# A four-layer graph network: engine orders from a repeating table, and the first three groups rearranged

## The chip, the core and the metric

One core of one Trainium2 chip runs the whole kernel. The time is the device time in microseconds (us) of one execution, and the median of several executions is compared. Five engines work side by side: TensorE (PE, matmuls and transposes into PSUM), VectorE (DVE), ScalarE (ACT), GpSimd (POOL) and SyncE (SP), whose queue issues all the DMAs of this kernel.

## The reference

128 graphs of 128 nodes with 512 features, float32, go through four layers. Each adds to x what its graph operation gives and normalises the rows.

```python
x = layernorm(x + relu(einsum('bnm,bmf,fc->bnc', dh * (A + I) * dh, x, W0) + b0))      # layer 0
q, k, v = x @ Wqk.T, x @ Wv.T          # layer 1: scores are masked by A and summed over a row,
x = layernorm(x + softmax(sum(q k^T / 8 * A, -1), axis=nodes) * v)
x = layernorm(x + relu(concat([x, (A @ x) / max(deg, 1e-6)]) @ W2.T))                  # layer 2
x = layernorm(x + L(A) @ (x @ W3 + b3))                                                # layer 3
```

## The kernel before

**Groups and layers.** Four graphs form a group, 32 groups in all (`NT`). Each group goes through the four layers; the loop at the end of the kernel function runs layer 0 and 1 of group t beside layer 2 and 3 of group t - 1, so a turn of that loop has one of each layer. `begin()` writes out groups 0 and 1, and group 2's layer 0, by hand.

**Products.** The weight products use a two-by-two scheme with seven products in place of eight, called B11, T1, B21, B22, T2, T3, T4. Sums of the left operand (`left_sums`, tiles agg0s, agg3s, xT1s) and of the weights (`outer_sums`, `weight_sums`) feed it. Layers 0 and 3 do it in `project` (PSUM tiles p_o), layer 1 in `l1_out` (p_v), and layer 2 applies the scheme twice, as four passes (`PASSES`) of seven products over accumulators p_2x, whose results are collected in the tiles y1 (its v) and y2 (its y). At the end of layer 2, `l2_out` writes for each of four graphs g a seed, y1 times a row factor, into a PSUM tile p_2g by ScalarE or VectorE, and TensorE adds the product of arT and y2 to it. Each product of two 128-row float32 tiles appears as two matmul records.

**Weights.** Layer 1's wv_sb and most of layer 2's (wb_sb, wa_sb, wc_sb) stay in SBUF. The tile wz_sb is shared in turn by layer 0's weights, the last part of layer 2's and layer 3's; after the first use each set is kept in DRAM (w0d, w2d, w3d) and `fetch` loads it in seven pieces, each of which waits for the last product that reads the old piece.

**What sets the order.** The kernel function calls recorders, and nothing is issued until `nc.emit()`. A `Plan` then holds all operations with an estimated duration. `schedule` works out for each one when it is due (`last`), going back from the end over its readers, and adds 100 ns times an entry of the hand-set table `EARLY`. `run` goes forward in planned time: on each engine it takes, among the operations whose inputs and buffers are there, the one that is due first. `MOVED` names operations that go to another engine than the one written down. The keys of both tables are made by `keys`: engine letter, tile name without the group number, and a count, so one entry holds for every group. The result is a fixed order of instructions on each engine; on the chip each engine runs its own in that order and waits on semaphores. Every instruction is recorded by one helper, so its line in the profile is always L460, and the tile names tell the rows apart.

**The start.** `load_weight` and `load_w2` fetch the weights, the latter by 64 small DMAs into wb_sb, wa_sb, wc_sb and wz_sb, once w0 and w3 have been stored. `w2_sums` forms layer 2's sums in these tiles and stores w2d. Layers 1 and 3 use weights whose output mean has been taken off (`centre`, `centre_row`), by VectorE reductions and subtractions on VectorE or GpSimd. `l1_out(0)` puts its result v1_0 in one of the three x buffers.

Of the kernel before, what the change touches and what calls it, by code (L numbers as in the profile page):

```python
# [32 lines left out]
STATS = False  # L33
EARLY = {
    "g:agg0:0": 86, "g:agg0s1:0": -9, "g:agg0s2:0": 119, "g:agg0s4:0": 323, "g:agg3:0": -34, "g:agg30:0": 49,
    "g:agg30s1:0": 93, "g:agg30s2:0": 80, "g:agg30s4:0": -89, "g:agg31:0": -413, "g:agg31s1:0": 10,
    "g:agg31s2:0": 251, "g:agg31s4:0": -88, "g:agg3s1:0": -120, "g:agg3s2:0": 22, "g:agg3s4:0": -318, "g:arT:0": 62,
    "g:arT:1": -359, "g:d:0": 569, "g:inner:0": -54, "g:inner:1": 47, "g:inner:2": -803, "g:inners1:0": 585,
    "g:inners1:1": -183, "g:inners2:0": 991, "g:inners2:1": -116, "g:inners4:0": -90, "g:inners4:1": 237,
    "g:last3o2_0:0": -956, "g:last3o2_0:1": -51, "g:last3o2_0:2": -224, "g:last3o3_0:0": -366, "g:last3o3_0:1": 433,  # L40
    "g:last3o3_0:2": -917, "g:last3o3_0:3": 629, "g:last3o3_1:0": -630, "g:last3o3_1:1": 138, "g:last4o2_0:0": 1012,
    "g:rs:0": -45, "g:rstdo0_0:0": 39, "g:rstdo0_0:1": -71, "g:rstdo0_1:0": -161, "g:rstdo0_1:1": 587,
    "g:rstdo3_1:0": 350, "g:rstdo3_1:1": 432, "g:v1_0:0": 318, "g:v1_0:1": 295, "g:v1_1:0": -218, "g:v1_1:1": -168,
    "g:v2_0:0": -165, "g:v2_1:0": 1445, "g:wa_sb": 56, "g:wb_sb": -132, "g:wc_sb": 200, "g:wz_sb": 303,
    "g:xT1:0": -225, "g:xT1s1:0": 1610, "g:xT1s2:0": 246, "g:xT1s4:0": -55, "g:xT2:0": -478, "g:xT2:1": -131,
    "g:xT2:2": 116, "g:xT2s1:0": 136, "g:xT2s1:1": -762, "g:xT2s2:0": -59, "g:xT2s2:1": 667, "g:xT2s4:0": -488,
    "g:xT2s4:1": -14, "s:agg0:0": -232, "s:agg0:1": 46, "s:agg0:2": -437, "s:agg0:3": 398, "s:agg3:0": -3638,
    "s:agg3:1": -430, "s:agg3:2": -69, "s:agg3:3": 136, "s:agg3:4": 61, "s:agg30:0": -153, "s:agg30:1": -305,
    "s:agg31:0": 172, "s:agg31:1": 228, "s:ana:0": -446, "s:arT:0": -3, "s:b0_sb": -185, "s:b3_sb": -253,
    "s:dme:0": -145, "s:e_sb": 2, "s:f_2x0:0": -26, "s:f_2x1:0": -284, "s:f_2x2:0": 3, "s:f_2x3:0": -1252,  # L50
    "s:f_o0:0": 120, "s:f_o3:0": -61, "s:f_o3:1": 1810, "s:f_v_0:0": 60, "s:f_v_1:0": 145, "s:p_2g_0:0": 165,
    "s:p_2g_1:0": 133, "s:p_2g_2:0": 589, "s:p_2g_3:0": 103, "s:p_2x0:0": -309, "s:p_2x0:1": 2768, "s:p_2x1:0": 477,
    "s:p_2x1:1": -115, "s:p_2x2:0": 130, "s:p_2x2:1": 233, "s:p_2x3:0": -185, "s:p_2x3:1": -154, "s:p_o0:0": -207,
    "s:p_o0:1": -24, "s:p_o0:2": 257, "s:p_o0:3": 252, "s:p_o3:0": -495, "s:p_o3:1": -134, "s:p_o3:2": -399,
    "s:p_o3:3": 29, "s:p_v_0:0": 37, "s:p_v_0:1": 427, "s:p_v_1:0": -59, "s:p_v_1:1": 655, "s:sa:0": 1, "s:sa:1": 48,
    "s:sa:2": -170, "s:sa:3": -253, "s:square_0_0:0": 219, "s:square_0_1:0": 177, "s:square_1_0:0": -251,
    "s:square_1_1:0": 474, "s:squareo2_0_0:0": -443, "s:squareo2_0_1:0": 848, "s:squareo2_1_0:0": -347,
    "s:squareo2_1_1:0": 201, "s:squareo3_0_0:0": -50, "s:squareo3_0_1:0": 457, "s:squareo3_1_0:0": 733,
    "s:squareo3_1_1:0": -12, "s:to_dram<x:0": 52, "s:to_dram<x:1": -172, "s:to_dram<x:2": -76, "s:to_dram<x:3": 324,
    "s:v0:0": 138, "s:v0:1": -520, "s:v0:2": -233, "s:v1:0": -335, "s:v1:1": 399, "s:v1:2": 544, "s:w0d": -498,  # L60
    "s:w2d": 281, "s:w3d": 433, "s:wa_sb": 198, "s:wb_sb": 162, "s:wc_sb": -241, "s:wqk_sb": 255, "s:wv_sb": -194,
    "s:wz_sb": 328, "s:x:0": -12, "s:x:1": 625, "s:x:10": -442, "s:x:11": 200, "s:x:12": 445, "s:x:13": -171,
    "s:x:14": 307, "s:x:15": -59, "s:x:2": 68, "s:x:3": 454, "s:x:4": -272, "s:x:5": -170, "s:x:6": -485,
    "s:x:7": 368, "s:x:8": 373, "s:x:9": 253, "s:xT1:0": 108, "s:xT1:1": -485, "s:xT1:2": 3, "s:xT1:3": -151,
    "s:xT1s_0:0": 153, "s:xT1s_0:1": -190, "s:xT1s_1:0": -127, "s:xT1s_1:1": -430, "s:xT1y_0:0": 64, "s:xT1y_0:1": 42,
    "s:xT1y_0:2": 135, "s:xT1y_0:3": 218, "s:xT1y_1:0": 141, "s:xT1y_1:1": -13, "s:xT1y_1:2": 15, "s:xT1y_1:3": 24,
    "s:xT2:0": 310, "s:xT2:1": 256, "s:xT2:2": 210, "s:xT2:3": 751, "s:xT2s_0:0": -40, "s:xT2s_0:1": 381,
    "s:xT2s_1:0": -191, "s:xT2s_1:1": -117, "s:xT2y_0:0": -236, "s:xT2y_0:1": -890, "s:xT2y_0:2": 317,
    "s:xT2y_0:3": 1574, "s:xT2y_1:0": 4, "s:xT2y_1:1": 244, "s:xT2y_1:3": 262, "s:y1:0": -50, "s:y1:1": -287,
    "s:ya:0": -330, "s:ya:1": -107, "s:ya:2": -697, "s:ya:3": 55, "t:p_2g_0:0": -246, "t:p_2g_1:0": 174,  # L70
    "t:p_2g_2:0": -200, "t:p_2g_3:0": 149, "t:p_2x0:0": 352, "t:p_2x0:1": 30, "t:p_2x0:2": 946, "t:p_2x0:3": -246,
    "t:p_2x0:4": 382, "t:p_2x0:5": 204, "t:p_2x0:6": 120, "t:p_2x1:0": 294, "t:p_2x1:1": 107, "t:p_2x1:2": -149,
    "t:p_2x1:3": -357, "t:p_2x1:4": -298, "t:p_2x1:5": 817, "t:p_2x1:6": 127, "t:p_2x2:0": -33, "t:p_2x2:1": 187,
    "t:p_2x2:2": 226, "t:p_2x2:3": 246, "t:p_2x2:4": -173, "t:p_2x2:5": 24, "t:p_2x2:6": -56, "t:p_2x3:0": 189,
    "t:p_2x3:1": 1006, "t:p_2x3:2": 223, "t:p_2x3:3": 320, "t:p_2x3:4": -136, "t:p_2x3:5": 237, "t:p_2x3:6": 356,
    "t:p_a0:0": 48, "t:p_a1:0": -152, "t:p_agg0_0:0": 635, "t:p_agg0_1:0": 403, "t:p_agg0_2:0": 31,
    "t:p_agg0_3:0": -384, "t:p_agg30_0:0": -152, "t:p_agg30_1:0": 248, "t:p_agg31_2:0": -11, "t:p_agg31_3:0": 68,
    "t:p_agg3_0:0": 766, "t:p_agg3_1:0": -517, "t:p_agg3_2:0": -889, "t:p_agg3_3:0": 242, "t:p_o0:0": 210,
    "t:p_o0:1": -990, "t:p_o0:2": 294, "t:p_o0:3": 1257, "t:p_o0:4": 676, "t:p_o0:5": 473, "t:p_o0:6": 579,
    "t:p_o3:0": -3306, "t:p_o3:1": 64, "t:p_o3:10": -240, "t:p_o3:11": -195, "t:p_o3:12": -175, "t:p_o3:13": 1090,  # L80
    "t:p_o3:2": -69, "t:p_o3:3": 207, "t:p_o3:4": 1976, "t:p_o3:5": 215, "t:p_o3:6": 645, "t:p_o3:7": 52,
    "t:p_o3:8": 187, "t:p_o3:9": 250, "t:p_sc:0": 107, "t:p_v_0:0": -764, "t:p_v_0:1": 308, "t:p_v_0:2": -150,
    "t:p_v_0:3": 906, "t:p_v_0:4": -231, "t:p_v_0:5": -802, "t:p_v_0:6": 596, "t:p_v_1:0": -87, "t:p_v_1:1": -8,
    "t:p_v_1:2": 90, "t:p_v_1:3": 180, "t:p_v_1:4": 470, "t:p_v_1:5": 19, "t:p_v_1:6": -34, "t:p_w:0": 358,
    "t:p_warm": 20, "t:p_ws:0": -194, "t:p_xT1_0:0": -130, "t:p_xT1_1:0": 78, "t:p_xT1_2:0": -45, "t:p_xT1_3:0": 18,
    "t:p_xT2_1:0": -3, "t:p_xT2_3:0": -198, "v:agg0:0": 260, "v:agg0:1": -192, "v:agg0s1:0": 27, "v:agg0s1:1": 117,
    "v:agg0s2:0": 240, "v:agg0s2:1": 22, "v:agg0s4:0": 43, "v:agg0s4:1": 281, "v:anT:0": 401, "v:anT:1": -116,
    "v:ana:0": -280, "v:ana:1": -301, "v:arT:0": -479, "v:b0_sb": 130, "v:b3_sb": -107, "v:bno0_0_0:0": 768,
    "v:bno0_0_1:0": 210, "v:bno0_1_0:0": 80, "v:bno0_1_1:0": -75, "v:bno3_1_1:0": 327, "v:bno3_1_1:1": -101,
    "v:deg:0": 422, "v:dh:0": -425, "v:dm:0": 236, "v:e_sb": 275, "v:inner:0": -237, "v:inner:1": 20,  # L90
    "v:inner:2": 994, "v:inner:3": -598, "v:last1o2_0:0": 466, "v:mean_b3": -42, "v:mean_w3": -128, "v:mean_wv": 4,
    "v:means_w3": 103, "v:means_wv": 26, "v:mn:0": 85, "v:mvo0_0:0": -254, "v:mvo0_0:1": 188, "v:mvo0_1:0": 20,
    "v:mvo0_1:1": 303, "v:mvo3_1:0": -173, "v:nhalf": 288, "v:nmro0_0:0": 447, "v:nmro0_1:0": -335, "v:rs:0": -240,
    "v:rsum:0": -3534, "v:scr:0": -701, "v:scr:1": 452, "v:scr:2": -222, "v:scr:3": -276, "v:u3:0": 240, "v:u3:1": 42,
    "v:u3:2": -40, "v:u3:3": 141, "v:u_o0:0": -207, "v:u_o0:1": 180, "v:v0:0": -35, "v:v0:1": -1085, "v:v1:0": 135,
    "v:v1:1": 201, "v:wa_sb": 617, "v:wc_sb": -873, "v:ws:0": -646, "v:wv_sb": -481, "v:wz_sb": -266, "v:x:0": -1020,
    "v:x:1": -470, "v:x:10": 202, "v:x:11": -70, "v:x:12": 283, "v:x:13": 906, "v:x:14": 576, "v:x:15": 293,
# [1282 lines left out]
```

## Time and profile before

| | us |
|---|---|
| median of 3 runs | 2434.84 |
| lowest and highest | 2434.82, 2438.7 |
| the profiled execution | 2437.22 |
| its span, first to last instruction | 2435.4 |

| engine | busy us of the span | share |
|---|---|---|
| PE | 2372.5 | 97% |
| DVE | 1761.9 | 72% |
| POOL | 1318.8 | 54% |
| ACT | 1138.6 | 47% |

The page also gives the 16 DMA engines' mean busy share, 59.9% for the main queue, and the TensorE clock granted, 0.995 of full speed on average. Its rows read: output tile, then what is read, with the shape, the count, the busy time, the mean of one in ns, and the idle time of the engine before them with what ended it. In the view in order of time a row has its start, its length, the engine and, in brackets, the idle time before it and its releaser. Matmul ends in the profile are modelled; their starts are not.

### The profile page before, as it was taken

The numbers are of one execution on the slowest core, as the hardware profiler recorded it, in microseconds if no ns is written. First come the engines' busy times: TensorE is split into PE (matmuls) and PEld (weight loads), VectorE is DVE, ScalarE is ACT, GpSimd is POOL, SyncE is SP. The second block draws the span as 40 slices with busy tenths as digits, with TensorE's granted clock in tenths as the row PEclk, the third lists the DMA queues.
The fourth block names the chain that finished last, engine by engine and source line by source line (L and its number), as shares of the span: only waits on it lengthen the run. The fifth ranks groups of instructions, "written<-read, shape, count | busy, mean of one in ns | idle before, by whom it ended". The sixth has DMA issues, their size and how long they took to land. (4 is left out here: it accounts for less than half of the span.)

```text
span 2435.4 us, 35420 instructions
## 1 busy us (share of the span) xinstructions
PE 2372.5 (97%) x11244; PEld 1923.1 (79%) x11244; DVE 1761.9 (72%) x3534; ACT 1138.6 (47%) x2495; POOL 1318.8 (54%) x1586
## 2 busy tenths in 40 slices
PE   7999999999999999999999999999999999999997
PEld 6677777887778887778877778877788777788776
DVE  7687777767777777777677777777776777776675
ACT  3344454444444444544444444445444445444444
POOL 3555556555555555565555555555655555655444
PEclk9999999999999999999999999999999999999999
DMA  5366656656566666565666566665666665665542
GB/s 165 122 168 186 176 160 201 176 165 191 166 180 185 176 172 192 154 195 173 172 187 170 172 191 174 172 194 158 184 183 169 187 174 161 201 175 161 171 117 75
DMA packets 490426, 417.36 MB, mean 171 GB/s; under 512 B 151808, under 2 KB 373504, under 8 KB 489856
## 3 DMA queue, kind: packets, MB, share of 16 engines
q1 hardware_dynamic: 490240, 415.09, 59.9%
q8 instruction: 91, 1.49, 0.3%
q14 instruction: 95, 0.78, 0.1%
HBM read 297.27 MB, written 117.70 MB: 170 GB/s over the span
## 5 line engine op out<-in xcount | busy, mean ns | idle before, releaser
L460 PE MATMUL p_o<-wz_sb,agg 128*128 128x256 f32 x2048 | 465.4, 379 | 3.4 <-DVE p_o L460 1.8
L460 PEld LDWEIGHTS p_o<-wz_sb,agg 128*128 128x128 f32 x2048 | 385.7, 190 | 56.2 <-DVE p_o L460 2.2
L460 PE MATMUL p_v<-wv_sb,xT 128*128 128x320 f32 x1024 | 296.3, 436 | 3.3 <-POOL wv_sb L460 2.6
L460 PEld LDWEIGHTS p_v<-wv_sb,xT 128*128 128x128 f32 x1024 | 195.6, 192 | 95.9 <-issue 9.8
L460 PEld LDWEIGHTS p_agg<-anT,x 128*128 128x128 f32 x2048 | 250.3, 193 | 23.7 <-DVE x L460 7.8
L460 PE MATMUL p_agg<-anT,x 128*128 128x128 f32 x2048 | 257.6, 277 | 7.8 <-DVE x L460 7.0
L460 PE MATMUL p_v<-wv_sb,xT1s 128*128 128x320 f32 x768 | 233.0, 433 | 0.0
L460 POOL TENSOR_TENSOR y<-u,y 128x1024 f32<-128x1024 f32 (+1 forms) x96 | 192.1, 2001 | 50.7 <-DVE y L460 40.9
L460 ACT COPY agg<-p_agg 128x512 f32<-128x512 f32 (+1 forms) x255 | 133.2, 535 | 164.9 <-PE p_agg L460 164.9
L460 PE MATMUL p_o<-wz_sb,agg0s 128*128 128x256 f32 x768 | 183.9, 383 | 6.6 <-DMA wz_sb<-w0d 5.7
L460 ACT COPY p_2x<-p_2x 128x512 f32<-128x512 f32 (+1 forms) x256 | 130.0, 518 | 127.2 <-PE p_2x L460 127.0
L460 PEld LDWEIGHTS p_v<-wv_sb,xT1s 128*128 128x128 f32 x768 | 139.7, 190 | 59.0 <-issue 14.4
L460 DVE TENSOR_TENSOR y<-p_2x,y 128x512 f32<-128x512 f32 (+1 forms) x256 | 159.4, 623 | 32.6 <-PE p_2x L460 21.5
L460 ACT ACTIVATE squareo<-x 128x512 f32<-128x512 f32 x127 | 80.3, 632 | 213.7 <-DVE x L460 213.5
L460 PE MATMUL p_o<-wz_sb,agg3s 128*128 128x256 f32 x744 | 176.1, 379 | 1.4 <-POOL agg3s L460 0.9
L460 DVE TENSOR_TENSOR v<-p_v,f_v 128x320 f32<-128x320 f32 x128 | 62.8, 492 | 153.0 <-PE p_v L460 142.1
L460 PEld LDWEIGHTS p_o<-wz_sb,agg0s 128*128 128x128 f32 x768 | 143.3, 190 | 36.5 <-DMA wz_sb<-w0d 17.6
L460 POOL TENSOR_TENSOR agg3s<-agg,agg3s 128x512 f32<-128x512 f32 x31 | 39.5, 1273 | 230.3 <-DVE agg L460 226.2
L460 PEld LDWEIGHTS p_o<-wz_sb,agg3s 128*128 128x128 f32 x744 | 138.8, 190 | 20.1 <-POOL agg3s L460 1.1
L460 POOL TENSOR_TENSOR xT<-xT 128x512 f32<-128x512 f32 (+1 forms) x96 | 104.8, 1092 | 83.6 <-DVE x L460 75.7
L460 PE MATMUL p_2g<-y,arT 128*128 128x512 f32 x256 | 127.5, 602 | 20.0 <-DVE p_2g L460 18.0
L460 ACT COPY f_2x<-p_2x 128x512 f32<-128x512 f32 (+1 forms) x128 | 68.2, 533 | 165.9 <-PE p_2x L460 165.9
(198 smaller groups left out, 5192.6 us busy)
## 6 DMA issues: line engine op xcount, KB each, us to landing
wz_sb<-w3d SPq DMA_DIRECT2D x224, 256.0 KB, 3.8
wz_sb<-w2d SPq DMA_DIRECT2D x217, 256.0 KB, 2.7
wz_sb<-w0d SPq DMA_DIRECT2D x210, 256.0 KB, 4.1
x<-in_x_dram SPq DMA_DIRECT2D x31, 1024.0 KB, 5.3
out_dram<-x SPq DMA_DIRECT2D x31, 1024.0 KB, 4.2
xT2s<-x SPq DMA_DIRECT2D x120, 256.0 KB, 3.0
xT2y<-xT2s SPq DMA_DIRECT2D x240, 128.0 KB, 4.0
xT1s<-x SPq DMA_DIRECT2D x120, 256.0 KB, 2.5
```

What stands on the lines that cost most here:

```text
L460: op.ins = getattr(getattr(self.nc, op.engine), method)(*[v.real() if isinstance(v, Ref) else v for v in args], **{k: v.real() if isinstan ...
```

## The change

It has four parts.

1. **Orders from a table.** A new table `TIMES` lists, for each engine, all operations of one group with a number, and `PERIOD` is 73637. For groups 3 to 29 an operation gets `due`, its number plus group times period. In `run`, among the operations that have a `due`, an engine may take only the one with the least; the others, of groups 0 to 2, 30 and 31 and of the weights, are still picked as before. Keys of `EARLY` and `MOVED` now end in a letter for groups 0, 1, 2, 30, 31 and for what belongs to no group, so that these have entries of their own; both tables are replaced. In groups 3 to 29, by `MOVED`, the first wide sum of y2 (y2:4) goes from VectorE to GpSimd, some copies and normalisations swap between ScalarE and VectorE, and some sums of left operands between VectorE and GpSimd.
2. **Groups 0 to 2.** Group 2 is prepared before layer 1 of group 0, and its layer 0 stands before layer 2 of group 0. v1_0 gets the tile "inner" in place of an x buffer.
3. **Layer 2's weights.** The fourth block is loaded into the tiles y2 and y1 of layer 2 instead of wz_sb, summed there and stored as w2d in two DMAs; wz_sb keeps layer 0's weights through group 2, and w2d is fetched for group 0 too.
4. **Centring.** ScalarE copies with a running sum take the means, and ScalarE adds the negative mean; wv is centred right after group 0's aggregation.

The warm-up transposes are issued in units of four, and an unused branch (`STATS`) goes. The core of the diff, without the tables:

```diff
+            if 3 <= t < last - 1 and TIMES:
+                op.due = TIMES[op.engine[:2]][keys[op][2:]] + t * PERIOD
...
+        bound = {e: sorted((op for op in self.ops if op.engine == e and op.due is not None),
+                           key=lambda op: (op.due, number[op])) for e in self.ENGINES}
...
         def ready(r, op):
+            if op.due is not None and bound[op.engine][0] is not op:
+                return None
...
     def load_w2():
-        for w, j, c, i in ((wb_sb, 0, 0, 0), (wa_sb, 0, 1, 0), (wc_sb, 0, 0, 1), (wz_sb, 0, 1, 1)):
+        z = [tp.tile([P, 2, 2, 2, H], FP, tag=tag, name=f"w2{tag}", bufs=1).rearrange("p a b c m -> p (a b c) m")[:, 0:7]
+             for tag in ("y2", "y1")]
+        for w, j, i in ((wb_sb[:, :, 0], 0, 0), (wa_sb[:, :, 0], 1, 0), (wc_sb[:, :, 0], 0, 1), (z[0], 1, 1)):
...
-        outer_sums(wz_sb, other)
-        keep(wz_sb, "w2d")
+        outer_sums(z[0], other)
+        outer_sums(z[1], other)
+        st["w2d", "kept"] = scratch.tile([P, 7, 2, H], FP, tag="w2d", name="w2d", bufs=1)
+        for i in range(2):
+            nc.sync.dma_start(st["w2d", "kept"][:, :, i], z[i], run=256)
...
+    def centre(blocks, name):
+        m = sp.tile([P, 2, 8], FP, tag="mean", name=f"mean_{name}", bufs=1)
         for c in range(2):
+            for j in range(4):
+                row = tp.tile([P, F], FP, tag="row", name=f"row_{name}", bufs=1)
+                nc.scalar.activation(row[:, 0:H], blocks(j, c), AF.Copy, accum_out=m[:, c, j:j + 1])
+        h = m[:, :, 0:4].rearrange("p c (h j) -> p j c h", j=2)
+        s = m[:, :, 4:6]
+        nc.gpsimd.tensor_tensor(s, h[:, 0], h[:, 1], ALU.add)
+        nc.scalar.mul(s, s, -1.0 / F)
+        for c in range(2):
+            for j in range(4):
+                nc.scalar.activation(blocks(j, c), blocks(j, c), AF.Identity, bias=s[:, c, j // 2:j // 2 + 1])
...
         l0_agg(0, nc.vector, ONE_BY_ONE)
+        centre(lambda j, c: wv_sb[:, c, j, 0:H], "wv")
         prep_rows(1)
...
         l1_turn(0, turn_on_tensor)
+        prep(2)
         l1_out(0, {(T3, 1): [lambda: l1_turn(1, turn_on_tensor)]})
         l1_out(1, {(T1, 0): [lambda: l1_scores(0)], (B21, 0): [lambda: l1_softmax(0)], (B22, 0): [lambda: l1_add(0)]})
+        l0_agg(2)
+        l0_out(2)
         finish_tails()
+        fetch("w2d", 0)
         l2_turn(0, turn_on_tensor)
-        prep(2)
         l2_out(0)
-        fetch("w0d")
         l1_scores(1)
         l1_softmax(1)
         l1_add(1)
-        l0_agg(2)
         l2_turn(1)
-        l0_out(2)
-        fetch("w3d")
+        fetch("w3d", 0)
```

Of the table, the entries around the end of layer 2 on TensorE (p_2x, pass and product number in the order B11, T1, T2, B21, T3, B22, T4; one period, 73637, lies between these and the p_v rows of the next group):

```diff
+        "p_2x2:4": 105305, "p_2x3:2": 106652, "p_2x2:3": 107063, "p_2x3:3": 107489, "p_2x3:1": 109715,
+        "p_2x3:4": 110820, "p_2x3:5": 111083, "p_2x2:6": 111326, "p_2x1:6": 111446, "p_2x3:6": 113308,
+        "p_2g_2:0": 118224, "p_2g_0:0": 119011, "p_2g_1:0": 119153, "p_2g_3:0": 120969, "p_agg3_1:0": 133557,
```

## Prediction, before the result was seen

> **What bounds the kernel now.** I read the page first: busy shares and the row of slices.
>
> ```profile
> PE 2372.5 (97%) x11244; PEld 1923.1 (79%) x11244; DVE 1761.9 (72%) x3534; ACT 1138.6 (47%) x2495; POOL 1318.8 (54%) x1586
> PE   7999999999999999999999999999999999999997
> ```
>
> TensorE (PE) is the bound in every slice but the first and last, so only time between matmuls can be won, and a delay elsewhere counts only if it reaches PE. Second, PE in order of time in a stretch of one turn. Each group needs one p_ws transpose, so its starts mark turns:
>
> ```profile
> L460 PE MATMUL p_ws<-ident,e_sb x1: 273/273/273, 215.4 to 215.4; 128*128 128x128 f32 x1
> ...
> L460 PE MATMUL p_ws<-ident,e_sb x1: 272/272/272, 2217.3 to 2217.3; 128*128 128x128 f32 x1
> ```
>
> These are groups 2 and 29: 27 turns in 2001.9 us, 74.14 us each. What must a turn cost? From starts of neighbouring rows a 256-wide record takes 0.216 us (two in 0.43), a 320-wide one 0.269 (four in 1.08), a 512-wide one 0.429, a 128-wide one 0.112. A turn has 112 records of p_o, 98 of p_2x, 56 of p_v, 64 of p_agg, 8 of p_2g, 8 of p_sc and two single transposes: 24.2 + 21.2 + 15.1 + 7.2 + 3.4 + 0.9 + 0.2 = 72.14 us. So 2.0 us of each turn is lost, 54 us in 27 turns. Where, in the turn from 289 to 363 us:
>
> ```profile
> 332.51 0.59 PE L460 MATMUL p_2x<-wz_sb,xT2s 128*128 128x256 f32 x2
> 333.13 0.70 PE L460 MATMUL p_2x<-wz_sb,inner 128*128 128x256 f32 x2
> 333.66 0.59 PE L460 MATMUL p_2x<-wz_sb,xT 128*128 128x256 f32 x2
> ...
> 337.11 1.02 PE L460 MATMUL p_2g<-y,arT 128*128 128x512 f32 x2
> 338.70 1.96 PE L460 MATMUL p_2g<-y,arT 128*128 128x512 f32 x4 [0.56 <-DVE p_2g L460]
> ```
>
> From 337.11 to 338.70 is 1.59 us for two records worth 0.86: 0.73 lost. From 332.51 to 333.13 is 0.62 for 0.43, and 0.10 more to the next row; all such delays among p_2x in this turn add up to 0.66. The rest sits at p_o. Third, the waits of PE over the span:
>
> ```profile
> PE p_2g L460 <- DVE p_2g L460: 18.0, 30, 1.7
> ...
> PE p_o L460 <- DMA wz_sb<-w0d: 5.7, 6, 1.2
> ```
>
> The first falls in practically every turn. The second is irregular: most turns last 73.8 to 73.9 us, others up to 75.0, and the mean of 74.14 puts some 0.3 us a turn on them. Why the second p_2g is late is seen in VectorE's (DVE) and GpSimd's (POOL) rows there:
>
> ```profile
> 333.59 0.68 DVE L460 TENSOR_TENSOR u<-p_2x,f_2x 128x512 f32<-128x512 f32 x1
> 334.30 0.76 DVE L460 TENSOR_SCALAR p_2g<-y,v 128x512 f32<-128x512 f32 x1
> 335.16 2.60 DVE L460 TENSOR_TENSOR y<-p_2x,y 128x512 f32<-128x512 f32 x4
> 337.80 0.75 DVE L460 TENSOR_SCALAR p_2g<-y,v 128x512 f32<-128x512 f32 x1
> ...
> 334.40 2.36 POOL L460 TENSOR_TENSOR y<-u,y 128x1024 f32<-128x1024 f32 x1
> ```
>
> The product that comes second needs the seed written at 337.80 to 338.55, behind four sums. Fourth, the start:
>
> ```profile
> 47.24 1.99 PE L460 MATMUL p_o<-wz_sb,agg 128*128 128x256 f32 x8 [0.79 <-DVE u_o L460]
> 53.31 0.86 PE L460 MATMUL p_xT<-ident,xT1y 128*128 128x128 f32 x4 [4.07 <-ACT xT1y L460]
> ...
> 61.85 6.71 PE L460 MATMUL p_v<-wv_sb,xT 128*128 128x320 f32 x14 [2.62 <-POOL wv_sb L460]
> ```
>
> ```profile
> 54.00:68.00 14.00, 9.62 (x24) 6.02 (x24) 5.65 (x10) 5.17 (x9) 9.76 (x7) 0.53 0.48 168
> ```
>
> PE has nothing left after layer 0 of group 1: layer 1 waits for the norm of x and for wv, whose mean is taken off late, and in the second view the clock stands at 0.53. From 49.0 to 93.4 (first p_2x) are 44.4 us; the matmuls in it are 96 records of p_v (25.8), 24 transposes (2.6) and p_sc, p_w, p_ws (1.1), 29.5. Lost: 14.9 us.
>
> **What the Trainium skill says.** "TensorE: Matmul & The Clock Gate", section "HAM oscillation", warns of PE gaps over about 3.4 us, after which the clock halves; the 4.07 us gap and 0.53 after it agree. "Perfetto Trace Analysis", section "Tensor Engine Instruction", says that matmul ends are estimated and that ACT and DVE are strict first-in first-out; the records of 0.59 us per pair with starts 0.43 apart agree, so I count from starts. "GPSIMD Engine Reference", section "Engine selection", has GpSimd about twice as slow as VectorE on two-input elementwise work; here 128x512 takes 1.27 us against 0.69, 128x1024 2.37 against 1.23 (y rows).
>
> **The change, part by part.** The sum stands against the profiled execution, 2437.2 us (span 2435.4, 1.8 around it), which is 2.4 above the median of 2434.84.
>
> *The table, groups 3 to 29.* It adds no matmul; the numbers in it only sort. I sorted it modulo the period. On PE, p_2g_2 and p_2g_0 (first rows of the pair, seeds done early) now come ahead of p_2g_1, which needs the late DVE seed: it is due 1.72 us after the first instead of 0.86, more than the 0.73 it was late. Gain 0.73. In layer 2, the products on one accumulator stand apart: in the last pass T2 is now followed by three products before T3, and T3 by three before T4; where T4 followed T3 by one product (0.19 + 0.10 lost) there are now 2.6 us for a 0.69 us sum and its hop. I take 0.50 of the 0.66 as gone. Against it: the sum of y that was DVE's (1.23) goes to POOL, at 2.37 by the nearest row, so four sums are in line there before the first p_2g. POOL has room from the end of pass 1's B22 to pass 3's (14 products, 11.2 us) for 2.37 + 2.37 + 1.27 + 1.0 for a power. The last sum is due: B22 of pass 3 ends, DVE still does a T1 sum (1.30, now ahead of it) and u (0.69), up to 2.1 us, then 2.37 on POOL: 4.5 us, while PE has three products and two of p_v, 2.58 + 2.15 = 4.7. Cover by a hair; a late transpose ahead of these shows as a new wait. Bounds: 0 and 1.0 us; I take 0.35 for this and other new waits. The wait on w0d stays: between the end of layer 3's T1, which frees the slot, and layer 0's T1 there are p_agg, p_ws and one product, 2.7 us as before. Behind w0d on SyncE's queue come the xT2s stores and the other w0d pieces, in the same order as now. Net 0.73 + 0.50 - 0.35 = 0.88 a turn, 23.8 us in 27. ScalarE and DVE swap a few copies at 0.6 to 0.7 us; both are idle over a quarter of the turn, so nothing.
>
> *Centring on ScalarE.* Off DVE: two reductions of 2.29, two minor rows per weight (0.16), 2 x 1.22 on wc, 1.3 for b3; off POOL 2 x 1.89. On ScalarE per weight: 8 copies with a sum and 8 identities of 256 wide. The trace has no such copy; the plain one is 0.37 and reading a sum 0.19, the bounds 0.37 and 0.82 (512 wide with its read). At 0.56 and 0.45: 8.1 us, with b3 and small rows 18.5 in all. ScalarE is busy 26 of 69 us from 20 to 89, so it fits; each single step can delay a norm by up to 0.56. wv lands by about 27 us and can be centred by 45, before its first use; DVE's queue ahead of the norms loses 5 to 8 us.
>
> *Group 2's layer 0 early.* v1 leaves the x buffers, so x_2 can load before layer 1; preparing moves 11 DMA issues (3 to 7 us of SyncE) ahead, past 64 loads of layer 2's weights that take 7.5 us per 16. Layer 0 of group 2 is 16 p_agg products and 28 of p_o, 3.6 + 12.1 = 15.7 us of PE work to lay into the gap and after it, and it keeps the clock up. One fetch of w0d goes (7 issues), one of w2d comes: no change.
>
> *Own tiles.* The fourth block of weights goes to the y2 and y1 tiles, which must be stored (5.7 us for w2d now, after the sums) before layer 2 writes its own y. Now that store is issued at 109; layer 2 then starts some 15 us later than 93 by the inserted work, and the sums free of wz can end by 95. I take no cost, bound 8 us.
>
> Of 14.9 us lost I take 11 as recovered, plus 1 of the delays before and after: 12, bounds 4 and 18. The end (6.96 us at the last norm, 1.2 and 1.69 at p_2g) has the same dependencies; hints may win 1.5.
>
> Sum: 2437.2 - 23.8 - 12 - 1.5 = 2399.9; less 2.4, **2397.5**.
>
> **The rivals.** *Stalls come back elsewhere* (0.17): the order wins 0.2 a turn, 5.4; 2437.2 - 5.4 - 13.5 - 2.4 = 2415.9. For: cover of 0.2 us at p_2g. Against: DVE and POOL are not the bound. The table doing nothing falls here too. *All stalls go* (0.13), w0d's too: 1.7 a turn, 45.9, start 16, end 3: 2369.9. *Start not won* (0.14): the store from y2 and y1 comes late and layer 2 stands instead: 2437.2 - 25.3 - 2.4 = 2409.5. *Slower* (0.06): the sum of y moved to POOL lands in front of the last one with no cover, so p_2g waits 2.37 - 0.1 = 2.27 in each turn: 27 x (2.27 - 0.88) = +37.5, less 13.5 and 2.4: 2458.8. It decides from 1.4 us of wait a turn; POOL's room of 11.2 us speaks against it.
>
> **How the numbers follow.** The forecast has 0.50; its own range is 2386 to 2408. From 2374 to 2422 all but about 0.08 (the best case), 0.06 (slower) and 0.05 (upper part of the first rival) is held. 0.2%, 4.9 us, is about what a measurement can tell from no change: every case but the slower one is faster by more, save a sliver of the first rival: 0.92, 0.02, 0.06.
>
> **What would show it.** Right: turns of about 73.3 us between p_ws starts; the p_2g wait on DVE gone; no PE gap over 3 us and a clock of 1.00 between 20 and 90 us. Wrong: a p_2g wait on POOL's y in every turn; layer 2 of group 0 waiting on a y copy or on weights; w0d waits in more turns than now.

## The result, and the profile after

The forecast of 2397.5 us was missed: the changed kernel takes 2433.23 us (median of 12 runs, 2429.65 to 2439.18) against 2435.62 for the kernel before (12 runs). The ratio is 0.9989, with an interval of 0.9980 to 0.9998: 2.4 us, less than the 0.2% that the prediction named as measurable. The profiled execution took 2434.35 us, with a span of 2432.53 (before: 2435.35).

First the page of the changed kernel: busy time and TensorE's row of slices.

```profile
PE 2357.1 (97%) x11244; PEld 1941.4 (80%) x11244; DVE 1879.8 (77%) x3714; ACT 1080.6 (44%) x2375; POOL 1306.0 (54%) x1573
PE   7989999999999999999999999999999999999997
```

TensorE still bounds all slices but the first and last. New is the 8 in the third slice (122 to 182 us). Next the starts of p_ws, which mark the turns. The sum of the forecast can be held against them, all in profiled executions (before: group 3 at 289.3, group 29 at 2217.3 us; after: 299.7 and 2215.8):

| stretch | forecast | measured |
|---|---|---|
| start, up to p_ws of group 3 | -12 | +10.4 |
| 26 turns, group 3 to group 29 | -22.9 (26 x 0.88) | -11.9 (26 x 0.46; 74.15 to 73.70 us a turn) |
| from there to the end of the span | -1.5 | -1.3 |
| sum | | -2.8 |

So two terms failed: half of the turns' gain is missing, and the start lost where it should have won. The marks share the loss out only roughly: eight p_o records of the first turn lie ahead of its mark in the changed kernel, so that about 1.7 us of the +10.4 is work done early and not time lost, and the turns win that much less.

**A turn.** The waits of TensorE over the span of the changed kernel (us in total, times, longest):

```profile
PE p_2g L845 <- DVE p_2g L845: 20.5, 26, 1.0
PE p_agg L845 <- DVE x L845: 8.5, 2, 7.0
PE p_o L845 <- DMA wz_sb<-w0d: 7.4, 11, 1.8
PE p_w L845 <- DVE scr L845: 5.1, 1, 5.1
```

The first line is the wait that the table was to remove. It was 18.0 us in 30 waits, and it is 20.5 in 26, one in practically each turn. A wait list leaves out short delays, so here is the time that a turn loses, counted from start to start: what lies between the starts of two neighbouring records beyond the price of a record in the prediction, put down to the matmul that comes late (us, mean of the 26 turns):

| late matmul | before | after |
|---|---|---|
| p_2x | 0.75 | 0.01 |
| p_2g | 0.80 | 0.98 |
| p_o | 0.49 | 0.67 |

The delays at p_2x are gone. Three rows of that kind, whose like stood 0.62 and 0.53 us apart before, now start 0.43 and 0.44 apart, where two records cost 0.43:

```profile
484.12 0.59 PE L845 MATMUL p_2x<-wz_sb,xT2s 128*128 128x256 f32 x2
484.55 0.59 PE L845 MATMUL p_2x<-wz_sb,inner 128*128 128x256 f32 x2
484.99 0.59 PE L845 MATMUL p_2x<-wz_sb,xT 128*128 128x256 f32 x2
```

The loss at p_2g has grown instead. TensorE, then VectorE, then GpSimd, in order of time in the turn of group 5 (start, length, instruction):

```profile
491.02 1.88 PE L845 MATMUL p_2g<-y,arT 128*128 128x512 f32 x4
493.71 1.10 PE L845 MATMUL p_2g<-y,arT 128*128 128x512 f32 x2 [0.81 <-DVE p_2g L845]
```

```profile
488.80 0.68 DVE L845 TENSOR_TENSOR y<-p_2x,y 128x512 f32<-128x512 f32 x1
489.40 1.52 DVE L845 TENSOR_SCALAR x<-x,last3o 128x512 f32<-128x512 f32 x1
490.85 1.93 DVE L845 TENSOR_TENSOR y<-p_2x,y 128x512 f32<-128x512 f32 x3
492.81 0.75 DVE L845 TENSOR_SCALAR p_2g<-y,v 128x512 f32<-128x512 f32 x1
```

```profile
488.25 2.39 POOL L845 TENSOR_TENSOR y<-u,y 128x1024 f32<-128x1024 f32 x1 [1.09 <-DVE u L845]
490.56 1.26 POOL L845 TENSOR_TENSOR anT<-anT,d 128x512 f32<-128x512 f32 x1
```

The order on TensorE is the predicted one: two products first, the one with VectorE's seed third. But between VectorE's sums stands a normalisation of x, which took 1.52 us, and so the seed is written 0.81 us too late. In both kernels it is the same instruction (x:13), put on VectorE by an entry that `MOVED` has before and after. Before it stood behind the seed:

```profile
485.37 0.75 DVE L460 TENSOR_SCALAR p_2g<-y,v 128x512 f32<-128x512 f32 x1
486.03 1.29 DVE L460 STREAM_TRANSPOSE xT<-xT1y 128x512 f32<-128x512 f32 x2
487.25 0.45 DVE L460 TENSOR_SCALAR x<-x,last3o 128x512 f32<-128x512 f32 x1
```

There it took 0.45 us and stood ahead of no seed. The table moves it ahead of the seed: modulo the period its number is 40291, the seed's (p_2g_1:0) 43646. There it runs into GpSimd's sum of 2.39 us.

**The start.** Busy time of each engine in five stretches (length, then PE, PEld, DVE, ACT and POOL with their records, the granted clock, DMA share and GB/s). The kernel before:

```profile
0.00:40.00 40.00, 33.95 (x194) 29.68 (x195) 25.24 (x48) 15.22 (x32) 14.93 (x22) 1.00 0.73 229
40.00:70.00 30.00, 20.76 (x78) 14.85 (x77) 17.84 (x31) 10.32 (x18) 16.11 (x14) 0.77 0.36 113
70.00:130.00 60.00, 56.21 (x247) 41.47 (x246) 47.30 (x90) 22.60 (x51) 30.81 (x37) 1.00 0.34 103
130.00:160.00 30.00, 28.09 (x145) 23.01 (x144) 24.47 (x55) 16.01 (x38) 13.23 (x21) 1.00 0.79 193
160.00:300.00 140.00, 138.54 (x660) 111.95 (x659) 102.91 (x205) 67.91 (x149) 78.77 (x88) 1.00 0.61 172
```

The changed kernel:

```profile
0.00:40.00 40.00, 28.45 (x134) 24.32 (x135) 18.46 (x38) 14.02 (x41) 13.86 (x21) 0.91 0.67 196
40.00:70.00 30.00, 28.54 (x144) 23.32 (x144) 27.34 (x50) 15.38 (x44) 16.04 (x18) 1.00 0.32 103
70.00:130.00 60.00, 58.03 (x283) 46.80 (x282) 45.66 (x90) 22.54 (x49) 29.01 (x29) 1.00 0.46 132
130.00:160.00 30.00, 19.34 (x88) 14.41 (x87) 23.71 (x59) 15.67 (x31) 15.97 (x20) 0.89 0.59 152
160.00:300.00 140.00, 135.21 (x641) 108.28 (x640) 106.86 (x212) 63.26 (x139) 69.92 (x81) 1.00 0.58 162
```

Read down PE: -5.5, +7.8, +1.8, -8.8, -3.3 us. The gap that the prediction looked at (40 to 70 us, clock 0.77) is gone, and the clock there is 1.00. It is more than paid for in two places where the prediction did not look, the first 40 us and the stretch from 130 to 160, in both of which the granted clock is now below 1. Up to 300 us PE has been busy 8.0 us less than before; the rest of the 10.4 us of the table is matmuls that last longer at the lower clock, and the work done early; the two were not told apart. TensorE in the second place, in the changed kernel:

```profile
136.60 3.70 PE L845 MATMUL p_2g<-y,arT 128*128 128x512 f32 x8 [1.23 <-POOL y L845]
145.38 0.38 PE L845 MATMUL p_w<-ident,w 128*4 128x128 f32 x1 [5.08 <-DVE scr L845]
147.27 2.08 PE L845 MATMUL p_agg<-anT,x 128*128 128x128 f32 x8 [1.51 <-DVE x L845]
```

In the kernel before, at this time:

```profile
139.16 0.27 PE L460 MATMUL p_w<-ident,w 128*4 128x128 f32 x1
139.27 1.89 PE L460 MATMUL p_o<-wz_sb,agg 128*128 128x256 f32 x8
141.42 0.30 PE L460 MATMUL p_ws<-ident,e_sb 128*128 128x128 f32 x1 [0.26 <-DVE e_sb L460]
141.56 1.95 PE L460 MATMUL p_o<-wz_sb,agg0s 128*128 128x256 f32 x8
```

Those p_o are layer 0 of group 2, the work that the change moved forward. After layer 2 of group 0 PE has to wait for its norm; before, this work lay there and covered it.

### The profile page after: what moved, and what is told of

It is laid out like the page before. It is cut to its first block, busy times and chain, and to the rows that moved or that the text cites. A ratio compares the mean times of both kernels' runs of the same rounds, so it can differ in the third digit from the quotient of the medians.

```text
span 2432.5 us, 35664 instructions
## 1 busy us (share of the span) xinstructions
PE 2357.1 (97%) x11244; PEld 1941.4 (80%) x11244; DVE 1879.8 (77%) x3714; ACT 1080.6 (44%) x2375; POOL 1306.0 (54%) x1573
## 4 chain that ended last, share of the span: by engine, by line
PE 89%; DVE 5%; DMA 4%; issue 1%; POOL 1%; SPq 1%; ACT 0%; POOLq 0%; ACTq 0%; DVEq 0%
PE p_o L845 29%; PE p_2x L845 26%; PE p_v L845 19%; PE p_agg L845 9%; PE p_2g L845 4%; DMA wz_sb<-w0d 2%; DVE y L845 1%; DVE x L845 1%; PE p_sc L845 1%; DVE p_2g L845 1%; SPq L845 1%; DMA xT2y<-xT2s 1%; DMA wz_sb<-in_L_gnn_kernel_dram 0%; DMA x<-in_x_dram 0%; PE p_xT L845 0%
## 5 line engine op out<-in xcount | busy, mean ns | idle before, releaser
L845 PE MATMUL p_o<-wz_sb,agg 128*128 128x256 f32 x2048 | 480.0, 380 | 6.1 <-DMA wz_sb<-w0d 1.9
L845 PE MATMUL p_v<-wv_sb,xT 128*128 128x320 f32 x1024 | 307.3, 433 | 0.0
L845 PEld LDWEIGHTS p_agg<-anT,x 128*128 128x128 f32 x2048 | 260.2, 196 | 34.3 <-DVE x L845 9.6
L845 PE MATMUL p_agg<-anT,x 128*128 128x128 f32 x2048 | 266.4, 281 | 13.0 <-DVE x L845 8.5
L845 PEld LDWEIGHTS p_v<-wv_sb,xT 128*128 128x128 f32 x1024 | 189.8, 190 | 91.3 <-ACT p_v L845 12.7
L845 POOL TENSOR_TENSOR y<-u,y 128x1024 f32<-128x1024 f32 (+1 forms) x92 | 184.8, 2008 | 50.5 <-DVE u L845 42.9
L845 POOL TENSOR_TENSOR agg3s<-agg 128x512 f32<-128x512 f32 x30 | 38.0, 1268 | 268.1 <-DVE x L845 263.4
L845 PE MATMUL p_2g<-y,arT 128*128 128x512 f32 x256 | 126.9, 602 | 22.7 <-DVE p_2g L845 20.5
L845 DVE SCALAR_TENSOR_TENSOR x<-b_sb,rs,x 128x512 f32<-128x512 f32 x128 | 95.6, 749 | 46.3 <-ACT agg L845 36.7
L845 ACT ACTIVATE squareo<-x,last1o 128x512 f32<-128x512 f32 x128 | 92.4, 722 | 60.3 <-DVE last1o L845 57.3
```

Of the source, the lines that this page charges most:

```text
L845: op.ins = getattr(getattr(self.nc, op.engine), method)(*[v.real() if isinstance(v, Ref) else v for v in args], **{k: v.real() if isinstan ...
```

## The experiments

A time is the median of a kernel's runs, a ratio that to the kernel before beside it. That one stayed between 2435.43 and 2436.16 us, so medians of different comparisons are set against each other too. "A turn" is the mean over the 26 turns between the p_ws of groups 3 and 29 in the profiled execution.

### Halves of the change: the table without the start, the start without the table

The first kernel is the one before with groups 3 to 29 ordered by the table, and the new entries for groups 30 and 31:

```diff
+            if 3 <= t:
+                keys[op] = f"+{op.engine[0]}:{w}:{n}" + {last - 1: "y", last: "z"}.get(t, "")
+                if t < last - 1:
+                    op.due = TIMES[op.engine[:2]][f"{w}:{n}"] + t * PERIOD
```

> The table for groups 3 to 29 (and the new hints for groups 30 and 31), with groups 0 to 2 as in the kernel before. If the two traces are read rightly, the table wins 0.45 us a turn over 27 turns, 12 us, and the end 1.4: about 13 us faster than before, 2422. If the table brings nothing and the small gain lies elsewhere: within 3 us of before, 2433 to 2437.

Measured: 2445.23 us, a ratio of 1.0035 (1.0023 to 1.0047). A turn takes 73.54 us, 0.62 less than before, so the table wins in the turns by itself; but the p_ws of group 3 comes at 311.0 us, 21.6 later than before. The lines of the wait list say where:

```profile
PE p_2g L932 <- DVE p_2g L932: 18.1, 25, 0.7
PE p_v L932 <- DVE xT1s L932: 10.6, 1, 10.6
```

The table fixes in which order groups 2 and 3 interlock; a start that ends in another order stands still at the joint, once, for 10.6 us in one wait. That is half of the 21.6; 16 p_o records more ahead of the mark are 3.5 of it, and the rest was not taken apart. The two halves are no sum. The first line shows that the table leaves the p_2g wait in place without the new start too.

The second kernel has the new start, and groups 5 to 29 by the old hints without the table:

```diff
-            if 3 <= t < last - 1 and TIMES:
-                op.due = TIMES[op.engine[:2]][keys[op][2:]] + t * PERIOD
+            if 5 <= t < last - 1:
+                keys[op] = "+" + keys[op]
```

> The new groups 0 to 2 (and the new hints up to group 4), with groups 5 to 29 ordered by the old tables, no table of orders. If the new start costs what the p_ws marks show, about 10 us slower than before, 2445. If the start brings the 12 us that the prediction gave it: 2423.

Measured: 2656.19 us, 1.0902 (1.0888 to 1.0916), a turn of 81.06 us. Every turn is worse, and the run says nothing of the start. One likely reason is that the old numbers in `EARLY` were found for one exact sequence and now have another one in front of them. But the run also differs in something else: the loads of w0d, w2d and w3d had a common hint in the kernel before (`s:wz_sb`, 328), and here their keys have other names, so they have none. How much of the 7 us a turn each of them costs is not shown.

### x:13 behind the seed

The theory for the turn: x:13, and nothing else in the table, makes the seed late. One number puts it behind the seed, on the same engine:

```diff
-        "x:13": 187565,
+        "x:13": 190950,
```

> The changed kernel with one number of the table moved, so that VectorE's normalisation of x (x:13) comes after the seed of p_2g_1 and not before it. Theory: this instruction is held up to 1.5 us by GpSimd's wide sum of y, and delays the seed that TensorE waits for; then the p_2g wait of 0.8 to 1.0 us a turn goes and the kernel is 22 to 26 us faster than the changed one, about 2409. Rival: the four sums of y1 alone make the seed late, and half of the wait or more stays: 2420 or above.

Measured: 2424.52 us, 0.9956 (0.9940 to 0.9971), 8.7 us under the changed kernel, a third of what was expected; a turn of 73.24. TensorE's waits:

```profile
PE p_agg L845 <- DMA x<-in_x_dram: 5.4, 9, 1.8
...
PE p_2g L845 <- DVE p_2g L845: 1.0, 1, 1.0
```

The p_2g wait is gone (20.5 to 1.0), and from start to start a turn loses 0.00 at p_2g where it lost 0.98. Only part of it reaches the time, since two new losses come up. Nine turns now wait for a load of x, which no turn of the changed kernel did (0.31 a turn at p_agg). That fits an x which is finished later, so that its buffer comes free later for the next load. And 0.28 a turn is lost at p_v, in delays of some 0.2 us that are too short for the list: the p_v at 493.33 waits for a transpose xT on VectorE, which now stands behind x:13. For x:13 is still long, VectorE and GpSimd around it:

```profile
491.02 0.76 DVE L845 TENSOR_SCALAR p_2g<-y,v 128x512 f32<-128x512 f32 x1
491.69 0.97 DVE L845 TENSOR_SCALAR x<-x,last3o 128x512 f32<-128x512 f32 x1
492.58 1.29 DVE L845 STREAM_TRANSPOSE xT<-xT1y 128x512 f32<-128x512 f32 x2
```

```profile
491.11 1.27 POOL L845 TENSOR_TENSOR ana<-ana,ident 128x512 f32<-128x512 f32 x1
```

GpSimd's instruction ends at 492.38, x:13 at 492.66: 0.28 us later. In the changed kernel GpSimd's sum ended at 490.64 and x:13 at 490.92, again 0.28 later. In the kernel before it started first, at 487.25, 0.22 ahead of GpSimd, and took 0.45. So it is not slowed in proportion: it ends a fixed time after GpSimd's instruction, however long that one lasts. All 26 of these normalisations that start under a sum of y in the changed kernel end 0.28 or 0.29 us after it, and so do the 24 of this run under its shorter instruction.

### x:13 on ScalarE

The other cure takes x:13 off VectorE and leaves its number in the table as it is: ScalarE has nothing to do there (in the changed kernel it is idle 3.68 us ahead of its seed at 492.81). One entry of `MOVED` goes:

```diff
-    "s:x:11b", "s:x:11y", "s:x:12b", "s:x:12c", "s:x:12y", "s:x:13", "s:x:13y", "s:x:14y", "s:x:2a", "s:x:2z",
+    "s:x:11b", "s:x:11y", "s:x:12b", "s:x:12c", "s:x:12y", "s:x:13y", "s:x:14y", "s:x:2a", "s:x:2z",
```

> The changed kernel with the normalisation x:13 left on ScalarE, where it was written, so that it is neither in front of VectorE's seed nor late for the store of the group. Theory: the p_2g wait goes as in e3, and e3's new wait of TensorE on the load of x, which comes from the store made later, does not appear; 0.7 to 0.95 us a turn, 19 to 25 us faster than the changed kernel, 2408 to 2414. Rival: shorter turns alone make the load of x late, and the gain stays near e3's 9 us, 2420 or above.

Measured: 2402.88 us, 0.9864 (0.9851 to 0.9878): 30.3 us under the changed kernel, with one instruction of a turn on another engine. A turn takes 72.52 us. VectorE, ScalarE and TensorE in the same turn:

```profile
486.13 2.66 DVE L845 TENSOR_TENSOR y<-p_2x,y 128x512 f32<-128x512 f32 x4
488.83 0.75 DVE L845 TENSOR_SCALAR p_2g<-y,v 128x512 f32<-128x512 f32 x1
```

```profile
484.51 2.56 ACT L845 ACTIVATE x<-x,last3o 128x512 f32<-128x512 f32 x4 [0.65 <-POOL last3o L845]
488.83 0.69 ACT L845 ACTIVATE p_2g<-y,v 128x512 f32<-128x512 f32 x1 [1.75 <-DVE y L845]
```

```profile
488.35 2.74 PE L845 MATMUL p_2g<-y,arT 128*128 128x512 f32 x6
```

Three products (six records) of p_2g follow each other without a wait, and a turn loses 0.00 us at p_2g. ScalarE has done its fourth normalisation long before, at 487.07. Group by group the distance of p_ws is 72.35 to 72.5 us in most turns. Run a second time, as the neighbour of a later experiment:

> The changed kernel with x:13 on ScalarE once more, the neighbour that e9 is read against on the same chip: 2400 to 2406 us, a ratio of 0.985 to 0.988 to the kernel before.

It gave 2405.12 us, 0.9873 (0.9859 to 0.9887), and in its profiled execution a turn of 72.80, the difference being waits on w0d (9.3 us in 13, against 2.6 in 4 in the first). So the edit is worth 28 to 30 us: 0.98 us a turn at p_2g in both, more or less what the loads of w0d give or take. This is the fastest kernel of the study; it beats the one before by 1.3 to 1.4%.

### The start: the adjacency first

First theory for the start: it loses because SyncE now issues b0's row ahead of the first adjacency; VectorE's first sum over it begins at 7.32 us, before at 3.72. In the changed kernel the first p_o starts at 18.54 us, before at 13.05. Two hints turn the order of the two loads round:

```diff
-    "s:ana:0a": -372,
+    "s:ana:0a": 372,
...
-    "s:b0_sb:0w": 206,
+    "s:b0_sb:0w": -100,
```

> The changed kernel with the load of group 0's adjacency issued first on SyncE's queue and the bias row after it, as before. Theory: the first product of p_o comes 5.5 us late because the adjacency lands at 7.0 us in place of 3.7 and the clock drops in the gap; then 4 to 5 us faster than the changed kernel, about 2428. Rival: VectorE's and GpSimd's order sets it, and the time stays within 1 us of 2433.

Measured: 2427.98 us, 0.9969 (0.9958 to 0.9981), 5.3 us under the changed kernel. That is the number expected, but the trace does not show why: the profiled execution has its p_ws of group 3 at 299.3 us and turns of 73.75, against 299.7 and 73.70. It took 2434.90 us and is the slowest of the six (the others 2426.54 to 2428.74), with one turn of 77.21, so it cannot show where the others gained. The edit with x:13 on ScalarE:

> e4 and e5 together. If the start and the repeating groups are independent, the two gains add: 5 us below e5, about 2405. Rival: the load of the adjacency shifts the later loads of the start and the gain of e4 is lost: within 2 us of e5.

Measured: 2403.97 us, 0.9869 (0.9856 to 0.9883), against 0.9864 (0.9851 to 0.9878) without it: nothing. The first p_o does start 2.0 us earlier there (16.51), and p_ws of group 0 only 0.6 (81.0 against 81.6); TensorE is busy 29.02 us of the first 40 against 28.46. The wait is passed on: PE still stands 1.5 us for an accumulator that VectorE prepares, 1.0 for its sums in wz and 1.35 for u_o. So the order of the loads explains the late first p_o in part, but here it does not shorten the start: p_ws of group 3 comes at 299.5 us, against 298.0. Where the 5.3 us between the medians of the other pair come from stays open.

### The start: the hole at 136 to 147 us

The 5.08 us ahead of p_w are put down to scr, which waits for the single tile that the squares of layer 2's norm use as well, and which stands behind them. If the scores of group 1 are written ahead of layer 2 of group 0, p_w has no such wait (on top of the adjacency's order):

```diff
-        l2_out(0)
         l1_scores(1)
         l1_softmax(1)
         l1_add(1)
+        l2_out(0)
```

> e4 with the scores, softmax and addition of layer 1 of group 1 written before layer 2 of group 0. Theory: with group 2's layer 0 used up early, TensorE has nothing to do after layer 2 of group 0 until the scores of group 1, which wait for the one row tile that the norm of layer 2 also uses; then its waits of 5.1 and 1.5 us go and the time is 5 to 7 us below e4, about 2422. Rival: the hole is layer 2's norm itself and only moves: within 2 us of e4, 2428.

Measured: 2455.60 us, 1.0081 (1.0067 to 1.0095), 27.6 us worse than without it, which neither the theory nor its rival had. The scores are early indeed (p_ws of group 1 at 107.1 us), but p_ws of group 3 comes at 321.6. TensorE's waits show new ones on other engines:

```profile
PE p_o L845 <- POOL agg0s L845: 7.3, 3, 4.3
...
PE p_2x L845 <- POOL last3o L845: 3.7, 1, 3.7
```

All three edits together:

> The edits of e4, e5 and e7 together. If they add: 2433 less 22, 5 and 6, about 2400, near the forecast of 2397.5. If they interfere, 2410 or above.

Measured: 2430.39 us, 0.9977 (0.9969 to 0.9986). It is about the sum of what was seen: turns of 72.58 us, as with x:13 on ScalarE, and p_ws of group 3 at 323.9.

The other way to close the hole is to put back into it what lay there, layer 0 of group 2. This needs w0d to be loaded once more, since wz_sb then holds layer 2's weights (x:13 is on ScalarE here):

```diff
         l0_agg(2)
-        l0_out(2)
         finish_tails()
         fetch("w2d", 0)
         l2_turn(0, turn_on_tensor)
         l2_out(0)
+        fetch("w0d", 2)
+        l0_out(2)
```

> The changed kernel with x:13 on ScalarE (2402.9 us, the run e5), and with one part of the start undone: the matmuls of group 2's layer 0 are written after layer 2 of group 0 again, as in the kernel before, with the extra load of w0d that this needs (wz_sb holds w2d by then). If moving this layer 0 forward only moved a hole, then the 7.8 us in which TensorE idles between 135 and 148 us (1.26 ahead of p_2g, 5.08 ahead of p_w, 1.51 ahead of p_agg) shrink to under 3, no hole of that size opens ahead of them, p_ws(3) comes at 290 to 293 us in place of 298.0, and the time is 2395 to 2399. If the work is wanted where the change put it (the gap at 47 to 95 us opens again without it), the 7.8 us go, but as much is lost ahead of 100 us, and the time stays within 3 us of 2403. If the reload of w0d and the orders that were tuned to the other sequence decide, new waits on wz_sb and on copies come up between 130 and 230 us and the time is 2408 to 2425.

Measured: 2427.00 us, 0.9952 (0.9938 to 0.9966), 21.9 us worse than its neighbour in the same comparison, nearest to the third of the expected cases; p_ws of group 3 at 319.8. The stretches of time, same columns as above:

```profile
0.00:40.00 40.00, 28.46 (x138) 24.28 (x139) 18.86 (x39) 13.80 (x41) 13.99 (x22) 0.91 0.63 186
40.00:70.00 30.00, 25.14 (x116) 20.31 (x115) 19.39 (x33) 13.28 (x38) 12.43 (x13) 0.89 0.32 115
70.00:130.00 60.00, 53.96 (x242) 40.21 (x240) 41.78 (x93) 23.16 (x50) 25.28 (x28) 0.94 0.45 135
130.00:160.00 30.00, 25.36 (x114) 19.28 (x115) 21.57 (x49) 12.88 (x26) 16.90 (x20) 1.00 0.49 131
160.00:300.00 140.00, 127.15 (x557) 99.09 (x557) 107.76 (x208) 56.92 (x123) 70.22 (x81) 0.98 0.59 172
```

Beside the kernel with x:13 on ScalarE and layer 0 where the change has it (28.46, 28.56, 58.02, 19.31 and 135.69 us of PE in these stretches), 6.1 us are won from 130 to 160, and p_w has no wait any more; but 3.4 are lost from 40 to 70, 4.1 from 70 to 130 and 8.5 after 160. So this work does fill the hole at 136 to 147 us when it lies there, and the time ahead of it then loses about as much. That the loss after 160 us, the largest of the three (a stop of 3.7 us at a p_2x at 200.24 is its largest piece), is owed to orders tuned to the other sequence is likely, but no run took it apart.

## Why the prediction was wrong, by its own steps

- **The bound, the turn's floor and what is lost in it** held. 72.14 us were worked out for a turn; with x:13 on ScalarE most turns take 72.35 to 72.5.
- **The failed step of the turn is "more than the 0.73 it was late. Gain 0.73", two products of p_2g ahead of the late seed.** The order on TensorE came as sorted, and it can do what was said of it: with x:13 off VectorE the wait falls from 18.0 us to 1.0. But the step took the seed to be as late as in the kernel before. It read TensorE's order out of the table, and not what the table puts ahead of this seed on VectorE. In the change as made the seed starts 1.79 us after the first p_2g, before 0.69; that is 1.10 later, more than the 0.86 that the new order gives, and the 0.80 us lost at p_2g became 0.98 in place of 0.07.
- **VectorE's and ScalarE's queues, "both are idle over a quarter of the turn, so nothing"**: this is where the seed's queue dropped out of the sum. It prices a queue by its mean load, while what counts is what stands in line ahead of the one instruction that TensorE waits for. x:13 is not one of the swapped instructions, since it is VectorE's in both kernels; the table alone puts it ahead of the seed. And it is longer there: not 0.45 us as before, but 1.5 (25 times in the span), because GpSimd held it. The two kernels that differ in x:13 alone give its price: 2433.23 - 2402.88 = 30.3 us, 28.1 in the repeat, and 1.17 and 0.90 us a turn. The Trainium skill has the mechanism: "SBUF — State Buffer", section "SBUF: two separate sides", says that VectorE in a two-port mode or with two SBUF inputs and GpSimd share one pair of ports under an exclusive lock, which the one that starts first keeps for its whole instruction. The end 0.28 us after GpSimd's instruction, whatever its length, and the 0.45 where VectorE was first, agree with it; that x:13 runs in such a mode is taken from its speed (0.48 us with nothing on GpSimd, against 0.75 for the seed of the same size, which writes to PSUM), and no run tested it. The prediction's "late transpose ahead of these" was the right kind of danger with the wrong instruction.
- **The distance of products on one accumulator, 0.50 of 0.66**: right; of the delays among p_2x (0.75 us a turn in the mean) 0.01 is left, so all of them went rather than three quarters.
- **The sum of y on GpSimd, 0.35 for new waits, and the rival of a slower kernel**: a wait on POOL's y does not come up in the turns, so the room of 11.2 us sufficed. The cost came from the same sum by another way, not through who waits for it but through the ports that it holds.
- **w0d stays**: right in kind; 5.7 us in 6 waits became 7.4 in 11, and between 2.6 and 9.3 in two runs of one kernel, so it moves from execution to execution.
- **Centring on ScalarE and the gap at 49 to 93 us, 11 of 14.9**: right where it looked. PE's time from 40 to 70 us grew by 7.8 at a clock of 1.00 in place of 0.77, the p_v wait on wv is gone, and a copy with the read of its sum comes every 0.54 us, a centring every 0.41, against 0.56 and 0.45 as priced.
- **The failed step of the start is "15.7 us of PE work to lay into the gap and after it": only the gap that it would fill was counted, not the one that it had been filling.** Layer 0 of group 2 lay behind layer 2 of group 0, and waits of 7.8 us stand at 136 to 147 there now; PE is busy 8.8 us less from 130 to 160. Put back, the work wins 6.1 us there, so this much is shown; that nothing is gained in all (21.9 us lost) leaves open what the best place would be. To this comes a loss in the first 40 us (5.5 us of PE's time), for which the prediction had named 5 to 8 us of relief on VectorE. The order of the first loads makes up 0.6 us of it (29.02 against 28.46), and turning it round brought 5.3 us in one pair of kernels and nothing in the other (2403.97 against 2402.88), so its part in the time stays open. That the rest is VectorE's chain of single steps, each of which PE waits for, is only what the trace suggests.
- **The store from y2 and y1**: w2d's store is issued at 97.94 us, earlier than the 109.19 of before. No wait of PE is put down to it. The rival "start not won" came true in what it said of the start, but not for its reason.
- **The end, -1.5**: measured -1.3; no run looked into why.

With x:13 on ScalarE the sum comes close to the forecast, but by luck: the turns gain 42.4 us, 1.63 each, where 0.88 had been taken with 1.7 as the best case, because the p_2x delays went completely and the reserve of 0.35 for new waits was not needed. The start takes 8.7 back where 12 was to be won, and the end gives 3.3; the errors cancel to within a microsecond.

## What to carry to other kernels

Where one engine is the bound, price a reordering by the queue ahead of each instruction that the bound engine waits for, not by the mean load of the engines: one normalisation of 0.45 us ahead of a seed cost 28 to 30 us in 27 turns. Before an instruction on VectorE is moved, look at what GpSimd runs at that moment; one that would be held belongs on ScalarE or ahead of GpSimd's start. When work is moved into a gap, ask what it covers where it lies now.

## What the runs showed of the hardware

A normalisation of 128x512 on VectorE (one SBUF input and a scalar) takes 0.48 us with nothing on GpSimd, and 0.44 to 0.45 where it starts 0.22 us ahead of GpSimd's instruction. It takes 1.52 when it meets a running sum of 2.39 us on GpSimd, and 0.97 when it meets an instruction of 1.27: it ends 0.28 us after GpSimd in both. VectorE's sums that read one operand from PSUM are not held: the one at 488.80 ran entirely beside the same sum on GpSimd and took 0.68 us, and none of the 192 of its kind in the changed kernel took more than 0.69. On ScalarE the same normalisation takes 0.71 us, longer than VectorE's 0.48, and was the better place.
